# A state-space layer's dt and dt x, repeated through HBM in one transfer each

## The chip, the cores and the metric

The kernel runs on one core of a Trainium2 chip. The metric is the device time of one execution in microseconds. Engines are named as in the profile: PE is TensorE (PEld its weight loads), DVE is VectorE, ACT is ScalarE, POOL is GpSimd, SP is SyncE, which issues most DMAs.

## The reference

A decoder layer on x of 8 sequences of 512 tokens with 512 features, all in float32: a state-space (Mamba) block, a cross attention with 16 heads, and a mixture of 32 experts, each followed by a layer norm. The change lies in the state-space block, with 1024 channels d and 16 states n for each:

```python
dt = softplus(dt @ dt_proj_w + dt_proj_b)
dA = exp(A * dt[..., None])
dBx = dt[..., None] * B_ssm[:, :, None, :] * x_main[..., None]

def scan_fn(h, inp):
    dA_t, dBx_t, C_t = inp
    h = dA_t * h + dBx_t
    y_t = einsum('bdn,bn->bd', h, C_t)
    return (h, y_t)
```

So each channel's dt is needed for its 16 decays, and each channel's dt x for its 16 inputs.

## The kernel before

**Tiling.** The program has three parts: `layers` (state-space block, attention, gate and shared expert), `experts`, and `finish`. `layers` walks over 16 chunks, each half a sequence (T = 256 tokens), two chunks to a sequence. Beside the scan of one sequence stands the attention and the gate of the sequence before it (`units`), cut into small parts, and the projections of the next chunk.

**A chunk** has 32 steps (q, g, jj): q is one of four groups of 256 channels, g one of four groups of states, jj one half of the channels of q. In a step a tile h of 128 partitions holds, on four partition groups of 32, four states of the same 32 channels, and along the free axis four times 32 channels by 256 tokens. So 512 such steps make the layer. A step is
- `steps_in` (L497, VectorE): h = dt x times B, with B broadcast along partitions in a tile bc;
- `scan` (L504, VectorE): the recurrence along the tokens, with the decays in l_da, of which there are two;
- `collect` (L513, VectorE): h times C, in place;
- `products` (L524, PE): sums over the states of the four partition groups into py, through a matrix fold;
- for the next step, `carry` (L491, ACT: the first column of a new h) and `decays` (L483, ACT: four exponentials of dt);
- `keep` (L509, ACT) copies the last states of the chunk's first half, for the second.

The tile h comes from a pool with four buffers: the `steps_in` of a step waits for the `products` of four steps back.

**dt and dt x.** `prepare` (L440 to L463) makes dt and dt x of a q with 256 channels: a matmul, four kinds of ACT instructions, then four VectorE instructions (L460 to L463). These tiles have the channels on partitions. Since h has four copies of 32 channels, `repeat` (L432) copies rows of 32 partitions, 64 KB at a time and from SBUF to SBUF, into four tiles rep of 128 partitions (dt and dt x, for jj = 0 and 1): eight copies for a tile, 32 for a q. Each of the four has one buffer. `prepare` of a q stands at step 3 of the eight steps of the q before it; the `repeat` of dt at steps 5 and 6, that of dt x at steps 6 and 7.

**B and C.** `x_proj` leaves them in a small HBM tensor scr; `bcast` (L419) reads a row of it into 32 partitions at once, four copies for a tile bc.

**Order.** The Python text gives an order for each engine in which `part` and `run` put the side work into thirds of a step; `wait` delays the second half of a part by a step. The framework places instructions on each engine's queue, and the order on a queue is fixed when the program is built. An engine or a queue waits at its first instruction that isn't ready. SP issues the copies in such an order, and each waits for the copy eight before it on one of eight semaphores.

Of the kernel before, what the change touches and what calls it, by code (L numbers as in the profile page):

```python
# [8 lines left out]
F32 = mybir.dt.float32  # L9
# [8 lines left out]
P = 128  # L18
# [6 lines left out]
NST = 16  # L25
RANK = 32
CC = DI // P
T = 256
NT_ = T // P
NG = NST // 4  # L30
NQ = 4
QP = P // NQ
NB = 4
NPB = 3

# [53 lines left out]
def layers(ctx, tc, a, x1d, filld, based, xbuf):  # L89
# [23 lines left out]
    nc = tc.nc  # L113

    mp = ctx.enter_context(tc.tile_pool(name="l_mamba", bufs=1))
# [7 lines left out]
    dp = ctx.enter_context(tc.tile_pool(name="l_dram", bufs=2, space=DRAM))  # L123
# [289 lines left out]
    def bcast(f, g):  # L413

        got = []
        for r0 in (g, NST + g):
            t = bcp.tile([P, T], F32, tag="bc", name="bc")
            for s in range(NQ):
                nc.sync.dma_start(  # L419
                    t[s * QP : (s + 1) * QP], f["scr"][r0 + s * NG, :].partition_broadcast(QP)  # L420
                )
            got.append(t.unsqueeze(1).to_broadcast([P, NB, T]))
        f["bc", g] = got

    def repeat(f, q, what, jj):

        to = mp.tile([P, 2, 2, T], F32, tag=f"rep{what}{jj}", name="rep")
        src = f["ready", q][what]
        for s in range(NQ):
            for j in range(2):  # L430
                r0 = (2 * jj + j) * QP
                nc.sync.dma_start(to[s * QP : (s + 1) * QP, j], src[r0 : r0 + QP])  # L432
        f["rep", what, q, jj] = to

    def prepare(q, f):

        ps = psm.tile([P, 2, T], F32, tag="mm", name="ps_dt")
        for i in range(2):
            c = 2 * q + i
            nc.tensor.matmul(  # L440
                ps[:, i, :], w_dt[:, c * P : (c + 1) * P], f["xd"][0:RANK, :], start=True, stop=True
            )

        def exponentials():
            u = mp.tile([P, 2, T], F32, tag="u", name="u")
            dt = mp.tile([P, 2, T], F32, tag="dt", name="dt")

            for i in range(2):
                c = 2 * q + i
                nc.scalar.activation(u[:, i, :], ps[:, i, :], AF.Abs, bias=b_dt[:, c : c + 1])  # L450
                nc.scalar.activation(dt[:, i, :], ps[:, i, :], AF.Relu, bias=b_dt[:, c : c + 1])  # L451
            nc.scalar.activation(u, u, AF.Exp, scale=-1.0)
            l = mp.tile([P, 2, T + 3], F32, tag="xp", name="l")[:, :, 0:T]
            nc.scalar.activation(l, u, AF.Ln, bias=1.0)
            w = dtx = mp.tile([P, 2, T], F32, tag="dtx", name="dtx")
            nc.scalar.activation(w, u, AF.Identity, bias=1.0)

            def both():

                nc.vector.scalar_tensor_tensor(w, w, -1.0, u, ALU.add, ALU.subtract)  # L460
                nc.vector.tensor_tensor(l, l, w, ALU.subtract)
                nc.vector.tensor_tensor(dt, dt, l, ALU.add)
                nc.vector.tensor_tensor(dtx, dt, f["xs"][q], ALU.mult)  # L463
                f["ready", q] = dt, dtx
                return wait(timesD)

            def timesD():
                for i in range(2):
                    c = 2 * q + i
                    nc.scalar.activation(  # L470
                        f["xs"][q][:, i, :], f["xs"][q][:, i, :], AF.Identity, scale=dpar[:, c : c + 1]
                    )

            return wait(both)

        return exponentials
# [10 lines left out]
    def carry(t, q, g, jj):  # L487

        last = state[:, q, g, jj].unsqueeze(2)
        h = mp.tile([P, NB, T + 1], F32, tag="h", name="h", bufs=4)  # L490
        nc.scalar.copy(h[:, :, 0:1], last if t else nothing)  # L491
        return h

# [12 lines left out]
    def keep(t, q, g, jj, h):  # L506

        if t < S // T - 1:
            nc.scalar.copy(state[:, q, g, jj].unsqueeze(2), h[:, :, T : T + 1])  # L509
# [565 lines left out]
    f = {"xt": x0}  # L1075
# [13 lines left out]
    n = 0  # L1089
# [6 lines left out]
    nc.vector.tensor_scalar(aneg, aneg, -1.0, None, ALU.mult)  # L1096
    decays(f, 0, 0, 0, das[0])
    ahead, products = carry(0, 0, 0, 0), None
    old, side, cleared = None, [], 0
    clock.append(0)  # L1100

    for i, (b, t) in enumerate(chunks):
        nf = {}
        after = chunks[i + 1] if i + 1 < len(chunks) else None
        if t == 0:
            side, spent = units(b - 1) if b else sources(0), 0.0

            own = [work(k) for k in range(len(steps))] * 2
            whole = sum(own) + sum(x[0] for x in side)
        for k, (q, g, jj) in enumerate(steps):  # L1110
            if i and k == 1:
                bcast(f, NG - 1)
            if after and 28 <= k < 31:
                bcast(nf, k - 28)
            qf, nq = (f, q + 1) if q + 1 < CC // 2 else (nf, 0)
            h = ahead

            parts = []

            def part(fn, *args, first=False):  # L1120
                parts.append((do, fn, *args, first))

            if k in (2, 3) and old:
                part(back, k - 2, *old)
            if 4 <= k < 8:
                part(gate_x, k - 4, f)
            if k == 8:
                parts.append((finish_silu, f["zs"]))
            if k % 8 == 3:
                if q + 1 < CC // 2:  # L1130
                    part(prepare, q + 1, f)
                elif after:
                    part(prepare, 0, nf)
            if after:
                if k == 10:
                    part(norm_x, nf)
                if k == 13:
                    for j in range(DC // 2):
                        part(flip_x, j, nf)
                if k in (14, 16, 19, 22):  # L1140
                    part(convolve, after[1], (14, 16, 19, 22).index(k), nf, first=(k == 14))
                if k == 24:
                    parts.append((finish_silu, *nf["xs"].values()))
                if k == 25:
                    part(x_proj, nf)
            if side and (k >= 4 or t and k < 2):
                at = t * len(steps) + k + 1
                while side and spent + sum(own[:at]) <= whole * at / len(own):
                    w, fn, alone = side.pop(0)
                    spent += w  # L1150
                    part(fn, first=alone)
            thirds = [[], [], []]
            for m, x in enumerate(parts):
                thirds[round((m + 0.5) * 3 / len(parts) - 0.5) if x[0] is do else 1].append(x)

            def run(m):
                clock[0] += 1
                settle()
                for x in thirds[m]:
                    if x[0] is do:  # L1160
                        do(*x[1:-1], first=x[-1])
                    else:
                        x[0](*x[1:])

            steps_in(f, q, g, jj, h)
            if g == NG - 1 and (qf is f or after):
                repeat(qf, nq, 1, jj)
            if k % 8 == 1:
                if k > 1:
                    gated(q - 1, f)  # L1170
                elif old:
                    gated(CC // 2 - 1, old[2])
            if i == 0 and k == 0:
                load("Wo")
            if i == 0 and k == 2:
                biases()
            if k == 0 and old:
                twice_x(*old)
            if k == 7 and after:
                load_x(*after, nf)  # L1180
            run(0)
            scan(das[n % 2], h)
            n += 1

            if k + 1 < len(steps) or after:
                then = steps[(k + 1) % len(steps)]
                ahead = carry(t if k + 1 < len(steps) else after[1], *then)
                decays(f if k + 1 < len(steps) else nf, *then, das[n % 2])
                if k % 8 in (5, 6) and (qf is f or after):
                    repeat(qf, nq, 0, k % 8 - 5)  # L1190
            keep(t, q, g, jj, h)
            run(1)

            if products:
                products()
            products = collect(f, q, g, jj, h)
            run(2)
            while i < 2 and cleared < E * (i * len(steps) + k - 6) // (2 * len(steps) - 7):
                clear(cleared)
                cleared += 1  # L1200
        while t and side:
            _, fn, alone = side.pop(0)
            do(fn, first=alone)
        old = (b, t, f)
        f = nf
# [356 lines left out]
```

## Time and profile before

| | |
|---|---|
| median of 3 runs | 5823.85 us (5821.39 to 5825.35) |
| profiled execution | 5829.17 us |
| its span, first to last instruction | 5827.5 us |
| state-space stage (77 to 3975 us) | 3898 us |
| rest (experts, finish) | 1852 us |
| PE busy in the span | 4844.7 us (83%) |
| DVE busy in the span | 4256.2 us (73%) |
| ACT busy in the span | 2571.1 us (44%) |
| copies of L432 | 2048 of 64 KB |
| copies of L419 | 512 of 32 KB |

The stage holds 16 chunks of some 244 us. A row "engine line <- releaser: us, times, longest" of the waits tells how long an engine stood still before an instruction of that line, and what ended it; "DMA rep<-dtx" is a copy that landed. In the time line an instruction's start and duration come first, and the idle time before it last, in brackets.

### The profile page before, as it was taken

Reading aid. Unit: us, or ns where it says so; the run is one execution under the profiler, and the core shown is the slowest. Engines: PE = TensorE matmul, PEld = TensorE weight load, DVE = VectorE, ACT = ScalarE, POOL = GpSimd, SP = SyncE. Lnnn points to the kernel's source line nnn. Section 1 sums busy time; section 2 is a strip of 40 time slices with the busy share of each in tenths; the row PEclk is TensorE's granted clock in tenths of the full one; section 3 lists DMA queues with packets and bytes.
Section 4 is the critical chain, followed back from the end, with each engine's and each line's share of the span. In section 5 each row is a group of like instructions: output and inputs, shape, how many; then the busy total and the mean of one; then the engine's idle time right before and its main releaser. Section 6 shows DMA issues by size and latency. Waiting matters only on the chain. (4 is left out here: it accounts for less than half of the span.)

```text
span 5827.5 us, 56423 instructions
## 1 busy us (share of the span) xinstructions
PE 4844.7 (83%) x17320; PEld 2526.6 (43%) x17320; DVE 4256.2 (73%) x5372; ACT 2571.1 (44%) x5688; POOL 524.8 (9%) x424
## 2 busy tenths in 40 slices
PE   5556878888888888887788787878899999999995
PEld 3122323323333333332343243233377777777773
DVE  5877879788787987988778798876355555555554
ACT  4444555556455455645545555553222222222223
POOL 0000002000100100010020010001111111111111
PEclk7767889898989899898898898989899999999997
DMA  5566335424533543362443354244234444444444
GB/s 163 157 209 188 97 96 144 139 73 116 171 81 101 153 126 84 107 185 60 118 147 110 90 142 140 70 102 138 84 98 125 125 121 121 123 121 122 122 121 145
DMA packets 517407, 719.33 MB, mean 123 GB/s; under 512 B 148097, under 2 KB 231585, under 8 KB 515056
## 3 DMA queue, kind: packets, MB, share of 16 engines
q1 hardware_dynamic: 481088, 627.28, 36.3%
q0 software_dynamic: 33280, 76.90, 6.8%
q10 hardware_dynamic: 2736, 11.54, 0.5%
q8 instruction: 138, 2.26, 0.2%
q14 instruction: 165, 1.35, 0.1%
HBM read 391.24 MB, written 165.05 MB: 95 GB/s over the span
## 5 line engine op out<-in xcount | busy, mean ns | idle before, releaser
L504 DVE TENSOR_TENSOR_SCAN h<-l_da,h 128x1028 f32<-128x1028 f32 x512 | 1167.0, 2289 | 62.7 <-ACT l_da L483 58.2
L483 ACT ACTIVATE l_da<-rep,l_aneg 128x256 f32<-128x256 f32 x2048 | 886.2, 498 | 364.7 <-DVE h L504 342.6
L524 PE MATMUL py<-h,l_fold 128*32 128x512 f32 x2048 | 462.5, 692 | 510.5 <-DVE h L513 450.2
L497 DVE TENSOR_TENSOR h<-rep,bc 128x1024 f32<-128x1024 f32 x512 | 613.1, 1215 | 277.4 <-DMA rep<-dtx 126.2
L513 DVE TENSOR_TENSOR h<-h,bc 128x1024 f32<-128x1024 f32 x512 | 619.9, 1217 | 5.2
L818 DVE TENSOR_REDUCE mx<-ps_s 128x2 f32<-128x1024 f32 x256 | 310.6, 1217 | 207.3 <-PE ps_s L816 188.1
L1312 PE MATMUL ps_h<-xT,w 128*128 128x320 f32 x1536 | 436.0, 433 | 0.0
L816 PE MATMUL ps_s<-l_ka,l_qa 64*128 64x512 f32 x1024 | 371.4, 731 | 59.9 <-DVE mx L818 58.8
L524 PEld LDWEIGHTS py<-h,l_fold 128*32 128x32 f32 x2048 | 62.3, 114 | 783.3 <-DVE h L513 388.2
L1392 POOL DMA_INDIRECT based<-y,xe x160 | 256.5, 1603 | 1309.1 <-ACT y L1415 580.7
L842 PE MATMUL ps_t<-l_qa,l_ka 64*128 64x512 f32 x1024 | 332.6, 669 | 46.1 <-DVE mx L818 17.8
L1312 PEld LDWEIGHTS ps_h<-xT,w 128*128 128x128 f32 x1536 | 292.6, 191 | 118.3 <-issue 0.6
L1333 DVE TENSOR_TENSOR hT<-ps_h,p 128x320 f32<-128x320 f32 x128 | 62.9, 492 | 379.0 <-PE ps_h L1312 379.0
L846 ACT ACTIVATE eT<-ps_t 128x1024 f32<-128x1024 f32 x256 | 260.2, 1017 | 152.1 <-PE ps_t L842 151.2
L858 PE MATMUL po<-eT,l_va 128*64 128x512 f32 x1024 | 307.2, 657 | 13.3 <-ACT eT L846 13.3
L1312 PE MATMUL ps_h<-t,s 128*128 128x320 f32 x1024 | 286.1, 432 | 0.0
L691 POOL DMA_INDIRECT xbuf<-x2t,dest x128 | 212.7, 1662 | 676.5 <-DVE dest L682 610.3
L509 ACT COPY l_state<-h 128x4 f32<-128x4 f32 x256 | 50.0, 195 | 498.4 <-DVE h L504 497.2
L555 PE MATMUL po<-wm,zs 128*128 128x512 f32 x512 | 250.1, 635 | 13.8 <-ACT nm L829 9.7
L753 PE MATMUL ps_p<-x2T,wa 128*128 128x512 f32 x512 | 248.4, 638 | 12.0 <-DVE hT L945 8.0
L344 PE MATMUL ps_x<-xnT,wm 128*128 128x256 f32 x1024 | 248.7, 397 | 5.4 <-ACT dt L451 3.1
L344 PE MATMUL ps_z<-xnT,wm 128*128 128x256 f32 x1024 | 238.7, 392 | 15.3 <-DMA wm<-in_in_proj_w 14.6
(230 smaller groups left out, 7465.2 us busy)
## 6 DMA issues: line engine op xcount, KB each, us to landing
w<-in_w SPq DMA_DIRECT2D x93, 1024.0 KB
wm<-in_in_proj_w SPq DMA_DIRECT2D x128, 512.0 KB
rep<-dt SPq DMA_DIRECT2D x1024, 64.0 KB
rep<-dtx SPq DMA_DIRECT2D x1024, 64.0 KB
xbuf<-zero SPq DMA_DIRECT2D x32, 1362.5 KB
xe<-xbuf SPq DMA_DIRECT2D x32, 1362.5 KB
wm<-in_out_proj_w SPq DMA_DIRECT2D x64, 512.0 KB
wa<-in_sw SPq DMA_DIRECT2D x24, 1024.0 KB
```

The source lines that it names most:

```text
L344: nc.tensor.matmul(ps[:, i, :], w[:, dc, i * P : (i + 1) * P], f["xnT"][:, dc, :], start=(dc == 0), stop=(dc == DC - 1),)
L483: nc.scalar.activation(da[:, n, 1:], dt[:, j, i, :], AF.Exp, scale=aneg[:, 2 * q + i, 2 * jj + j, g : g + 1])
L497: nc.vector.tensor_tensor(h[:, :, 1:], dtx.rearrange("p j i t -> p (j i) t"), f["bc", g][0], ALU.mult)
L504: nc.vector.tensor_tensor_scan(flat, da.rearrange("p n t -> p (n t)"), flat, 0.0, ALU.mult, ALU.add)
L513: nc.vector.tensor_tensor(h[:, :, 0:T], h[:, :, 1:], f["bc", g][1], ALU.mult)
L524: nc.tensor.matmul(f["py"][j * QP : (j + 1) * QP, :, :], fold, hs[j // 2][:, 2 * (j % 2) : 2 * (j % 2) + 2, 0:T], start=False, stop=g == N ...
L816: nc.tensor.matmul(ps[:, j, :], qa[r, lt * P : (lt + 1) * P], ka[r, :], start=True, stop=True)
L818: return lambda: nc.vector.tensor_reduce(mx[:, lt, :].unsqueeze(2), ps, AX.X, ALU.max) and None
L842: nc.tensor.matmul(ps[:, j, :], ka[r, kc * P : (kc + 1) * P], qa[r, :], start=True, stop=True)
L846: nc.scalar.activation(eT, ps, AF.Exp)
L858: nc.tensor.matmul(po[j * 2 * HD : (j + 1) * 2 * HD, :], va[:, kc, i, j * HD : (j + 2) * HD], eT[:, j, :], start=(kc == 0), stop=(kc == SC ...
L1312: nc.tensor.matmul(ps, w[:, n, r * P : (r + 1) * P], x[:, n, :], start=not more and n == 0, stop=n == 1, skip_group_check=more,)
```

## The change

- `repeat` reads from HBM: when `prepare` has made dt and dt x, each is stored to HBM in two copies (one for each jj), and `repeat` then fills a tile rep of 128 partitions with one copy, whose source has a step of 0 over the four partition groups. Its four calls for a q now stand at steps 5 and 6.
- The tiles rep share five buffers, in turn, instead of one for each of four names.
- `bcast` fills a tile bc with one copy, whose source has the four groups of states in front and a step of 0 over 32 partitions.
- `prepare` stands at step 2 of eight (for the first q of the next chunk still at step 27 of the chunk).
- h has five buffers.
- `keep` of a step is called a step later, after the next step's `carry` and `decays`.

```diff
         for r0 in (g, NST + g):
             t = bcp.tile([P, T], F32, tag="bc", name="bc")
-            for s in range(NQ):
-                nc.sync.dma_start(
-                    t[s * QP : (s + 1) * QP], f["scr"][r0 + s * NG, :].partition_broadcast(QP)
-                )
+            src = f["scr"].rearrange("(n s g) t -> n g s t", n=2, s=NQ)[r0 // NST, r0 % NST]
+            nc.sync.dma_start(t, src.unsqueeze(1).to_broadcast([NQ, QP, T]))
...
-        to = mp.tile([P, 2, 2, T], F32, tag=f"rep{what}{jj}", name="rep")
-        src = f["ready", q][what]
-        for s in range(NQ):
-            for j in range(2):
-                r0 = (2 * jj + j) * QP
-                nc.sync.dma_start(to[s * QP : (s + 1) * QP, j], src[r0 : r0 + QP])
-        f["rep", what, q, jj] = to
+        f["rep", what, q, jj] = to = mp.tile([P, 2, 2, T], F32, tag="rep", name="rep", bufs=5)
+        src = f["ready", q][what][jj]
+        nc.sync.dma_start(
+            to.rearrange("p j i t -> p (j i t)"),
+            src.rearrange("c j f -> c (j f)").unsqueeze(0).to_broadcast([NQ, QP, 4 * T]),
+        )
...
-                f["ready", q] = dt, dtx
+                f["ready", q] = [dp.tile([2, QP, 2, 2 * T], F32, tag=n, name=n) for n in ("dtd", "dtxd")]
+                for to, src in zip(f["ready", q], (dt, dtx)):
+                    for r in range(2):
+                        nc.sync.dma_start(
+                            to[r].rearrange("c j f -> j c f"), src[r * HP : (r + 1) * HP].rearrange("p i t -> p (i t)")
+                        )
...
-        h = mp.tile([P, NB, T + 1], F32, tag="h", name="h", bufs=4)
+        h = mp.tile([P, NB, T + 1], F32, tag="h", name="h", bufs=5)
...
-            if k % 8 == 3:
-                if q + 1 < CC // 2:
-                    part(prepare, q + 1, f)
-                elif after:
-                    part(prepare, 0, nf)
+            if k % 8 == 2 and q + 1 < CC // 2:
+                part(prepare, q + 1, f)
+            if k == 27 and after:
+                part(prepare, 0, nf)
...
-            if g == NG - 1 and (qf is f or after):
-                repeat(qf, nq, 1, jj)
+            more = qf is f or after
+            if k % 8 == 6 and more:
+                repeat(qf, nq, 0, 1)
...
-                if k % 8 in (5, 6) and (qf is f or after):
-                    repeat(qf, nq, 0, k % 8 - 5)
-            keep(t, q, g, jj, h)
+                if k % 8 == 5 and more:
+                    repeat(qf, nq, 0, 0)
+                    repeat(qf, nq, 1, 0)
+                if k % 8 == 6 and more:
+                    repeat(qf, nq, 1, 1)
+            if held:
+                keep(*held)
+            held = t, q, g, jj, h
             run(1)
```

More of the change, by code (lines that the diff above doesn't have):

```diff
@@ L32 @@
 QP = P // NQ
+HP = P // 2
 NB = 4
@@ L1098, in layers @@
     ahead, products = carry(0, 0, 0, 0), None
-    old, side, cleared = None, [], 0
+    old, side, cleared, held = None, [], 0, None
     clock.append(0)
```

## The prediction

> **What bounds the kernel now.** I read the window sums first, to find the stage that the change touches; then VectorE's waits in it; then the time line around the longest of those waits. The change lies between 77 us (first scan product) and 3975 us (last scan). The windows of that stage and of the expert stage (columns: window, us, busy us and instructions of PE, PEld, DVE, ACT, POOL, granted clock, DMA share, GB/s):
>
> ```profile
> 77.00:3975.00 3898.00, 3057.89 (x10228) 1281.86 (x10230) 3219.52 (x3439) 2023.02 (x4566) 229.72 (x197) 0.87 0.43 125
> 3975.00:5827.00 1852.00, 1744.54 (x6956) 1216.47 (x6952) 1018.00 (x1884) 518.89 (x1064) 284.37 (x190) 0.97 0.45 121
> ```
>
> VectorE works 3220 of 3898 us, TensorE 3058: VectorE paces the stage, TensorE is close behind, and 678 us of VectorE's time is idle. A chunk (32 steps) takes 243.6 us, a step 7.6 us, of which a scan (2.29 us) and its two products (1.22 us each) are 4.7. VectorE's waits in the stage (total us, times, longest):
>
> ```profile
> DVE mx L818 <- PE ps_s L816: 144.7, 50, 10.0
> DVE h L497 <- DMA rep<-dtx: 126.2, 14, 25.2
> DVE h L497 <- PE py L524: 117.0, 62, 6.1
> DVE h L504 <- ACT l_da L483: 58.2, 31, 6.3
> ...
> DVE h L497 <- PE ps_p L753: 22.4, 2, 11.6
> ...
> DVE h L497 <- issue: 5.7, 1, 5.7
> DVE h L497 <- DMA rep<-dt: 5.4, 3, 4.9
> ```
>
> The waits at L497 other than for py stand at the starts of a q, where the repeated dt and dt x arrive: 159.7 us in all. One of them on VectorE and on SP's queue:
>
> ```profile
> 1545.96 0.67 DVE L463 TENSOR_TENSOR dtx<-dt,xs 128x512 f32<-128x512 f32 x1
> ...
> 1559.17 1.22 DVE L497 TENSOR_TENSOR h<-rep,bc 128x1024 f32<-128x1024 f32 x1 [11.27 <-DMA rep<-dtx]
> ```
> ```profile
> 1549.65 1.78 SPq L432 DMA_DIRECT2D rep<-dt  x3
> 1551.84 4.95 SPq L432 DMA_DIRECT2D rep<-dtx  x8
> ...
> 1558.23 3.23 SPq L432 DMA_DIRECT2D rep<-dt  x5
> ```
>
> Eight 64 KB copies cost SP 5 us, and a q needs four such groups: dt x is ready at 1546.6 and its first half is there at 1559.2, 12.6 us later. By the landing records in the trace a 64 KB copy lands 2.0 us after its issue, a 128x512 store to HBM 2.0 to 2.8, a 512 KB weight tile 4.5. The same start in odd chunks shows as a 10.0 us wait of mx for ps_s. Over a pair of chunks (eight q) these waits are 11.3 + 4.0 + 2.2 + 1.3 + 4.9 + 10.0 = 34 us.
>
> **The change part by part.** Only this stage changes; VectorE's and ScalarE's arithmetic stays.
>
> *SP's issues.* 2048 copies of 0.59 us (L432) become 256 stores and 256 reads; 512 row broadcasts become 128. SP is relieved of some 900 us of issue. That is worth nothing by itself: it counts only through when data arrive.
>
> *When they are needed.* From the instruction order of the changed program and the durations above, VectorE's work between the dt x product and the first product that needs it (the cover) is, for the eight q of a pair from an even chunk's q = 1, 6.9, 10.4, 19.5, 9.1, 1.6, 16.2, 20.6, 6.8 us (before: 1.6, 15.8, 16.0, 19.5, 2.3, 17.6, 16.9, 14.2). The second product, which needs the other half, stands 2.5 us later. `prepare` a step earlier thus gives 5 us at one q and takes some elsewhere.
>
> *How long the new path takes: the row.* No row shows such a store and read. Nearest: two stores issued (0.7), landed (2.0 to 2.8), a read issued (0.6) and landed (4.5): 8 us after the dt x product. The stalls of a pair would be 1.1 + 0 + 0 + 0 + 6.4 + 0 + 0 + 1.2 = 9 us instead of 34.
>
> *The rule against it.* The Trainium skill, "DMA: Bandwidth & Descriptors", section "Why a DMA increments its semaphore by 16 and not by 1", says that a copy runs on at most 16 engines, and on the largest number up to 16 that divides the slowest dimension of both access patterns; its "Rules for kernel authors" warn of just this case, "a leading zero-stride broadcast of c copies". The built patterns: a read has source [4 copies, 32, 1024], so 4 engines; a store has destination [2, 32, 512], so 2; a row broadcast has source [4, 32 copies, 256], so 4. All copies of before had 32 or 128 in front. This trace agrees as far as it can: the six l_ka<-l_ones copies, with 4 in front, add to their semaphore once and then four times singly, where rep's copies add sixteen times. But those have only four rows, so no row shows many rows on four engines.
>
> By the rule the sum is another. An undisturbed packet of 2048 bytes takes 84 ns in this trace, one of 4096 bytes 159 ns. A store is 64 rows on 2 engines, 32 x 84 ns = 2.7 us on each; a read is 128 rows on 4 engines, 32 x 159 = 5.1 us. They share the first engines of one queue, so they follow each other there. With dt ready at 0, dt x at 1.0, and 1.65 us of fixed latency (2.0 less a 64 KB copy's four packets): stores end at 4.4, 7.1, 9.8, 12.5; reads at 17.6, 22.7, 27.8, 32.9. So the first half of dt x lands 21.7 us after the dt x product, the second 31.9. What stands between in SP's order (weight tiles 1.4 us each on an engine, attention rows) adds 1.4 to 4; the other traffic's share of an engine, 0.43 of the window less 0.13 for rep and bc (65,536 packets of 110 ns and 16,384 of 51 ns on 16 engines in 3898 us), would stretch 31.9 to 46 if it fell evenly. I take 35, near the lower end, since that traffic comes in bursts. Stalls of a pair at 35, with covers 2.5 us longer than above: 25.6 + 22.1 + 13.0 + 23.4 + 30.9 + 16.3 + 11.9 + 25.7 = 169 us.
>
> I take the rule: the page is specific, its count agrees with the small copies, and the built patterns are exactly those that it names. Its price is the likeliest, the row's is a rival.
>
> *Five h, later copies of the last states.* Before, the write to h waits 117 us for the py matmul four steps back; a fifth buffer puts the awaited matmul a step, some 5 us of VectorE's work, further back; between nothing and all 117 I take 65, as PE stays late at its own lumps. The held copy no longer makes ScalarE wait for the scan (497 us, mostly time in which ScalarE had nothing else); for VectorE I count at most 20 of its 58 us on l_da. What is late next is ps_s and py. When VectorE stalls 20 us at a q, TensorE catches up, and part of these gains and of the other waits (678 - 160 - 70 - 117 = 331 us, 41 a pair) is inside the stall; I take 20 of them and 8 of py a pair.
>
> *SP waits.* A read waits for its store, and behind it on SP stand weight tiles, kd/qT rows, nm and x1d; all use the crowded engines too. Demand on engine 0 for a q: four reads 20.4, four stores 10.8, two row broadcasts 3, others 0.30 x 61 = 18 us, together 52 of 61 us: tight, not yet the bound. Weight tiles are loaded three ahead and attention rows two head pairs ahead, which covers 15 to 20 us; without it TensorE would wait inside VectorE's stall.
>
> *Sum against the profiled execution (5829.2 us; span 5827.5).* A pair: +169 - 34 - 8 - 20 = +107; eight pairs +860. The first pair has DMA shares of 0.60 and 0.65 from the clearing of xbuf: +60 more. The start is about even (before, the first product comes 28 us after dt x; here some 32). Together +920: 6749, and as the median of the runs lies 5 us below the profiled time, 6745.
>
> **The rivals.**
> 1. *All 16 engines serve the new copies* (0.11). For it: no row of before contradicts it, and SP's issue, the visible cost, falls. Then 160 + 70 (mx) - 70 (stalls of 9 us a pair) + 65 + 20 = 245 us are freed; TensorE works 200 of 243.6 us a chunk, so a third returns as waits for it: -165, 5660 us. This ends faster. The deciding point is the landing of the second half: at 21 us after the dt x product the stalls are 60 us a pair, about what goes with the old path (34) and what is gained or lies inside the stalls (28). Below it faster, above it slower.
> 2. *Only the reads are confined, the stores are spread* (part of 0.87). Stores then take 3 us, the second half lands at 24.5: stalls 85 a pair, 85 - 62 = +23 a pair, with the first pair's 60 about 6070 us.
> 3. *The first engines become the bound* (part of 0.87). If the other traffic stretches the path to 45 us, the stalls are 249 a pair, 249 - 62 = +187 a pair: about 7300 us and TensorE starts to wait for wm.
> 4. *Gains and stalls cancel* (0.02).
>
> **How the numbers follow.** Confined engines 0.87, of which the middle case is the likeliest: 6745. Spread over 16: 0.11. The range runs from rival 2 to a little above rival 3, 6050 to 7400; it leaves out rival 1 and a tail of long queueing. Runs of before lie within 4 us of each other, so 0.2% (12 us) can be told. Faster 0.10, same 0.02, slower 0.88.
>
> **What would show it.** Right: waits "DVE h L497's product <- DMA rep<-dtxd" of over 1000 us in the stage, some 20 us at nearly each of 64 q, most at an odd chunk's q = 1; VectorE's busy time unchanged at 3220 us in a longer stage; expert stage still 1852 us; DMA share not above 0.43, though transfers are late; lower TensorE share. Wrong: reads that land within 6 us of their issue, and L497's waits under 100 us.

## The result, and the profile after

The changed kernel takes 6572.4 us (median of 4 runs, 6567.1 to 6579.6) against 5824.6 us (4 runs): ratio 1.1282, 95% interval 1.1263 to 1.1302. The profiled execution took 6572.3 us, 743 us more than that of before. The same parts of the page and of the window sums as before; the windows are cut so that the second is as long as before (the last scan ends at 4703 us, 15 us ahead of that cut):

```profile
PE 4969.2 (76%) x17320; PEld 2562.1 (39%) x17320; DVE 4224.3 (64%) x5372; ACT 2560.6 (39%) x5700; POOL 513.7 (8%) x424
...
HBM read 525.46 MB, written 198.61 MB: 110 GB/s over the span
```
```profile
83.00:4718.00 4635.00, 3185.06 (x10236) 1317.63 (x10237) 3186.99 (x3437) 2011.83 (x4574) 226.93 (x202) 0.82 0.35 112
4718.00:6570.00 1852.00, 1741.82 (x6947) 1215.06 (x6945) 1014.38 (x1880) 518.20 (x1064) 276.12 (x185) 0.97 0.46 120
```

From the first scan product to the end of the last scan the stage grew from 3899 to 4621 us, 722 of the 743 us; it starts 5 us later, and what follows the last scan takes 1868 us instead of 1851. VectorE's busy time in the stage did not grow (3187 us in the first window, before 3220), so its idle time did: 1448 us instead of 678. The DMA share fell from 0.43 to 0.35: on average over the 16 engines there is more room than before, while VectorE waits for copies. VectorE's waits (us in total, times, longest):

```profile
DVE h L500 <- DMA rep<-dtxd: 1078.4, 118, 23.1
DVE z L963 <- DMA based<-z: 102.8, 6, 19.3
DVE h L500 <- PE py L527: 72.6, 32, 6.9
...
DVE mx L821 <- PE ps_s L819: 47.1, 12, 7.7
DVE h L507 <- ACT h L494: 33.0, 7, 5.8
...
DVE h L507 <- ACT l_da L486: 8.2, 7, 2.8
```

L500 is the product that was L497. Its wait for dt x was 126 us and is 1078. The second row is new: a store of another part of the layer, z to HBM, now holds VectorE. Others shrank (ps_s 145 to 47, py 117 to 73, l_da 58 to 8), which fits that they lie inside the long waits. ScalarE stands as long for the copies of dt:

```profile
ACT l_da L486 <- DMA rep<-dtd: 1144.7, 124, 21.5
```

That is not what holds VectorE: its scan waits only 8 us for l_da, as dt x lands later than dt. One start of a q on VectorE and on SP's queue:

```profile
2092.21 0.69 DVE L460 TENSOR_TENSOR dt<-dt,l 128x512 f32<-128x512 f32 x1
...
2095.09 0.67 DVE L461 TENSOR_TENSOR dtx<-dt,xs 128x512 f32<-128x512 f32 x1
...
2119.18 2.36 DVE L500 TENSOR_TENSOR h<-rep,bc 128x1024 f32<-128x1024 f32 x2 [22.15 <-DMA rep<-dtxd]
...
2129.90 1.23 DVE L500 TENSOR_TENSOR h<-rep,bc 128x1024 f32<-128x1024 f32 x1 [6.15 <-DMA rep<-dtxd]
```
```profile
2092.96 1.20 SPq L465 DMA_DIRECT2D dtd<-dt  x2
...
2095.78 2.59 SPq L465 DMA_DIRECT2D dtxd<-dtx  x2
2098.42 1.50 SPq L428 DMA_DIRECT2D rep<-dtd  x1
2106.36 0.56 SPq L428 DMA_DIRECT2D rep<-dtxd  x1
2107.03 0.51 SPq L428 DMA_DIRECT2D rep<-dtd  x1
2108.93 1.21 SPq L428 DMA_DIRECT2D rep<-dtxd  x1
```

dt x is ready at 2095.8. SP issues the first read of it at 2106.4, after its store has landed, and all four reads by 2110. The first product starts at 2119.2 and the first one of the second half at 2129.9, 34 us after dt x. So the time goes into the copies themselves. Over the steady part (q 8 to 63) the trace's semaphore records give these means, from the dt x product on: stores landed after 6.7 (dt) and 13.3 us (dt x), the first half of dt x after 26.0, the second after 37.8. In the kernel before the two halves were there after 14.9 and 26.6 us.

The same records tell how many engines carry a copy. A read (rep) adds 5 times to its semaphore, a store 3 times, a row broadcast (bc) 5 times; the copies that had 32 or 128 rows in front add 16 times. The first addition of a dt x read comes 1.0 us after its issue, the other four 13 us and later (medians). Read as one addition at the issue and one for each engine, this is 4, 2 and 4 engines.

The copies that are still spread over 16 engines show the same without that reading. In the kernel before, the 16 additions of a store of z come between 2.1 and 2.6 us after its issue (in order, medians over the stores with all 16 on record). In the changed kernel twelve come after 5.3 to 5.4 us, two after 12 and two after 18. So four engines are late, and two of them later still: this is what to expect if the 2 engines of the stores are among the 4 of the reads.

### The profile page after: what moved, and what is told of

The parts are those of the page before. It is cut to its first block, busy times and chain, and to the rows that moved or that the text cites. A ratio compares the mean times of both kernels' runs of the same rounds, so it can differ in the third digit from the quotient of the medians.

```text
span 6570.6 us, 53769 instructions
## 1 busy us (share of the span) xinstructions
PE 4969.2 (76%) x17320; PEld 2562.1 (39%) x17320; DVE 4224.3 (64%) x5372; ACT 2560.6 (39%) x5700; POOL 513.7 (8%) x424
## 5 line engine op out<-in xcount | busy, mean ns | idle before, releaser
L500 DVE TENSOR_TENSOR h<-rep,bc 128x1024 f32<-128x1024 f32 x512 | 616.2, 1215 | 1164.4 <-DMA rep<-dtxd 1078.4
L845 PE MATMUL ps_t<-l_qa,l_ka 64*128 64x512 f32 x1024 | 356.6, 762 | 294.4 <-ACT eT L849 234.4
L527 PE MATMUL py<-h,l_fold 128*32 128x512 f32 x2048 | 428.1, 661 | 174.4 <-DVE h L516 141.1
L819 PE MATMUL ps_s<-l_ka,l_qa 64*128 64x512 f32 x1024 | 333.4, 724 | 204.0 <-DVE mx L821 188.5
L861 PE MATMUL po<-eT,l_va 128*64 128x512 f32 x1024 | 345.4, 754 | 65.2 <-ACT eT L849 51.2
L558 PE MATMUL po<-wm,zs 128*128 128x512 f32 x512 | 281.1, 707 | 144.6 <-DVE z L963 122.5
L345 PE MATMUL ps_z<-xnT,wm 128*128 128x256 f32 x1024 | 259.3, 413 | 81.8 <-ACT zs L391 60.0
L756 PE MATMUL ps_p<-x2T,wa 128*128 128x512 f32 x512 | 262.5, 668 | 58.7 <-ACT hT L950 50.9
L845 PEld LDWEIGHTS ps_t<-l_qa,l_ka 64*128 64x128 f32 x1024 | 113.0, 222 | 464.7 <-ACT eT L849 277.4
L345 PEld LDWEIGHTS ps_z<-xnT,wm 128*128 128x128 f32 x1024 | 208.9, 208 | 155.8 <-ACT zs L391 72.5
L819 PEld LDWEIGHTS ps_s<-l_ka,l_qa 64*128 64x128 f32 x1024 | 92.3, 206 | 391.0 <-DVE mx L821 285.9
```

What stands on the lines that cost most here:

```text
L345: nc.tensor.matmul(ps[:, i, :], w[:, dc, i * P : (i + 1) * P], f["xnT"][:, dc, :], start=(dc == 0), stop=(dc == DC - 1),)
L500: nc.vector.tensor_tensor(h[:, :, 1:], dtx.rearrange("p j i t -> p (j i) t"), f["bc", g][0], ALU.mult)
L527: nc.tensor.matmul(f["py"][j * QP : (j + 1) * QP, :, :], fold, hs[j // 2][:, 2 * (j % 2) : 2 * (j % 2) + 2, 0:T], start=False, stop=g == N ...
L558: nc.tensor.matmul(pos[j], yg[:, c, j * P : (j + 1) * P], w[:, i, :], start=(c == 0), stop=(c == CC - 1))
L819: nc.tensor.matmul(ps[:, j, :], qa[r, lt * P : (lt + 1) * P], ka[r, :], start=True, stop=True)
L845: nc.tensor.matmul(ps[:, j, :], ka[r, kc * P : (kc + 1) * P], qa[r, :], start=True, stop=True)
```

## The experiments

Line numbers shift by a few between kernels. In what follows "the product" is that of `steps_in`.

**1. All three copies spread over 16 engines, the way through HBM kept.** Channels and states stay where they were in the partitions; the copies are cut so that 32 rows stand in front.

```diff
-        nc.sync.dma_start(
-            to.rearrange("p j i t -> p (j i t)"),
-            src.rearrange("c j f -> c (j f)").unsqueeze(0).to_broadcast([NQ, QP, 4 * T]),
-        )
+        for s in range(NQ):
+            nc.sync.dma_start(
+                to[s * QP : (s + 1) * QP].rearrange("p j i t -> p (j i t)"), src.rearrange("c j f -> c (j f)")
+            )
...
-                        nc.sync.dma_start(
-                            to[r].rearrange("c j f -> j c f"), src[r * HP : (r + 1) * HP].rearrange("p i t -> p (i t)")
-                        )
+                        for j in range(2):
+                            r0 = r * HP + j * QP
+                            nc.sync.dma_start(to[r][:, j, :], src[r0 : r0 + QP].rearrange("p i t -> p (i t)"))
```

(The row broadcasts go back to four copies each.)

> The changed kernel with each of its new copies cut so that 32 rows stand in front on both sides: a tile rep by four reads of 32 rows of 4 KB, a tensor by four stores, a tile bc by four copies; the way through HBM, the five tiles rep and h and the later keep stay. Theory (few engines serve the new copies): all of them now run on 16 engines, each should add to its semaphore sixteen times, the first half of dt x lands some 8 to 12 us after the dt x product instead of 26, the waits of L500's products for rep fall from 1078 us to under 200, and the time is 5600 to 5800 us. Rival (the way through HBM, a store that has to land before a read starts, is itself the cost): 6300 us or more.

Measured: 6046.5 us, ratio to before 1.0369 (1.0351 to 1.0386). VectorE's waits in its stage:

```profile
DVE mx L823 <- PE ps_s L821: 166.8, 61, 10.4
DVE zs L543 <- ACT zs L396: 141.5, 9, 21.6
DVE xs L379 <- ACT xs L371: 123.7, 38, 13.1
...
DVE h L502 <- DMA rep<-dtxd: 27.9, 4, 13.0
```

The wait for dt x falls from 1078 to 28 us, as the theory said, and all these copies now add 16 times. But the first half of dt x is there after 16.8 us, not 8 to 12, and the time is in neither range: other waits, for TensorE and ScalarE, come up, and the kernel is 4% slower than before. With the engines spread the waits for rep are gone, yet this kernel, with 16 reads for a q, loses time in another way, and late work elsewhere probably hides part of what rep would still cost. Experiments 2 and 8 bear on it.

**2. The same engines with few copies: channels interleaved.** Channel c and state s go to partition 4c + s instead of 32s + c. Then the source of a read has 32 channels in front and the 4 repeats behind, and one copy goes to 16 engines. `fold` and the layout of A follow; the row broadcasts have 32 in front as well; the stores are cut as in experiment 1.

```diff
-            src.rearrange("c j f -> c (j f)").unsqueeze(0).to_broadcast([NQ, QP, 4 * T]),
+            src.rearrange("c j f -> c (j f)").unsqueeze(1).to_broadcast([QP, NQ, 4 * T]),
```

> Partition 4c + s instead of 32s + c: the source of a read is 32 channels in front, then a step of 0 over four, so a tile rep and a tile bc are still filled by one copy, on 16 engines; the stores are cut in four of 32 rows. VectorE's instructions stand in the same order as in spread_stores, so the two differ only in the engines of the reads. Theory: 5600 to 5750 us, as fast as spread_all or faster, for SP issues fewer copies. Rival (the way through HBM): 6300 us or more. Rival (a single large copy is slow because of its size): as slow as spread_stores.

Measured: 5429.6 us, ratio to before 0.9315 (0.9300 to 0.9331): faster than both kernels, and than the theory's range. Its page's engines, and VectorE's waits in the stage:

```profile
PE 4738.2 (87%) x17320; PEld 2491.1 (46%) x17320; DVE 4217.5 (78%) x5372; ACT 2560.8 (47%) x5703; POOL 542.1 (10%) x424
```
```profile
DVE h L501 <- DMA rep<-dtxd: 74.3, 20, 10.9
DVE h L501 <- PE py L528: 61.0, 22, 7.5
...
DVE mx L822 <- PE ps_s L820: 37.9, 24, 4.6
```

A read of dt x lands 6.1 us after its issue (median; 18 in the changed kernel), a cut store 1.7. The two halves of dt x are there 11.6 and 16.5 us after the product that makes it (26.0 and 37.8 in the changed kernel). The way through HBM, the five tiles, the earlier prepare and the single reads are all still there. What changed is the order of the dimensions and the cut of the stores.

**3. Stores alone spread** (experiment 1's edit to the stores, reads and row broadcasts as in the changed kernel, on 4 engines).

> The changed kernel with its stores alone cut in four of 32 rows (16 engines); reads and row broadcasts stay on four. Theory: stores land some 3 us after the dt x product instead of 13.3; four reads of 5.1 us follow each other on the same engines, so the first half of dt x lands after about 14 us and the second after 25; some half of the loss goes: 5950 to 6200 us. Rival (the way through HBM): within 100 us of 6570.

Measured: 6081.5 us, ratio 1.0429 (1.0411 to 1.0446), inside the theory's range, though the halves of dt x are there later than it had them, after 20.2 and 31.8 us. VectorE, ScalarE and TensorE have the same instructions in the same order as in experiment 2, so the step from here to experiment 2, 652 us, is the price of reads and row broadcasts on 4 engines instead of 16.

```profile
DVE h L500 <- DMA rep<-dtxd: 707.4, 103, 17.7
```

**4. Stores alone confined:** experiment 2 with the changed kernel's two stores for each tensor.

```diff
-                        for j in range(2):
-                            r0 = r * HP + j * QP
-                            nc.sync.dma_start(to[r][:, j, :], src[r0 : r0 + QP].rearrange("p i t -> p (i t)"))
+                        nc.sync.dma_start(
+                            to[r].rearrange("c j f -> j c f"), src[r * HP : (r + 1) * HP].rearrange("p i t -> p (i t)")
+                        )
```

> The interleaved kernel (channel c and state s in partition 4c+s; reads and row broadcasts on 16 engines; 5430 us) gets back the changed kernel's stores, two copies for each of dt and dt x with 2 in front of 32 rows, thus on 2 engines. With the changed kernel (stores 2, reads 4: 6572 us), the one with spread stores (16, 4: 6081 us) and the interleaved one (16, 16: 5430 us) it completes a square. Theory (the copies of the few engines follow each other there, so the cost is the sum of rows ahead of the last half, less the cover by other VectorE work): stores alone end 8.8 and 11.5 us after dt x, reads of 5 us then land at 14 and 17 us, against covers of 6.9, 10.4, 19.5, 9.1, 1.6, 16.2, 20.7, 6.8 us that makes some 35 us a pair of chunks, 280 in all, less the 77 us of rep waits that the interleaved kernel has: 5600 to 5750 us. Rival (the two losses add up): 5430 + 491 = about 5920 us. Rival 2 (the reads' engines alone matter): 5430 to 5480 us.

Measured: 5745.4 us, ratio 0.9856 (0.9839 to 0.9872), inside the theory's range.

```profile
DVE h L501 <- DMA rep<-dtxd: 296.7, 42, 14.6
```

The square is complete (device us; waits of the product for dt x in brackets):

| | reads on 4 engines | reads on 16 |
|---|---|---|
| stores on 2 engines | 6572 (1078) | 5745 (297) |
| stores on 16 | 6081 (707) | 5430 (77) |

Spreading the reads is worth 827 or 652 us, the stores 491 or 316. ("Reads" includes the row broadcasts.) The effects are not additive: waiting that one copy causes is partly shared with the other. Along each row VectorE and ScalarE have the same instructions in the same order, so there the engines of the copies are the whole difference for them. Down a column the built order differs too (some 4,600 of VectorE's 5372 instructions stand in the same order), so 491 and 316 hold that as well.

**5. The suspected cost doubled:** experiment 3 with each tile filled by two copies that have 2 in front.

```diff
-        nc.sync.dma_start(
-            to.rearrange("p j i t -> p (j i t)"),
-            src.rearrange("c j f -> c (j f)").unsqueeze(0).to_broadcast([NQ, QP, 4 * T]),
-        )
+        for s in range(0, NQ, 2):
+            nc.sync.dma_start(
+                to[s * QP : (s + 2) * QP].rearrange("p j i t -> p (j i t)"),
+                src.rearrange("c j f -> c (j f)").unsqueeze(0).to_broadcast([2, QP, 4 * T]),
+            )
```

> The kernel with the stores in four copies of 32 rows (6081 us) is changed in one thing: each tile rep is filled by two copies whose source has 2 copies in front of 32 rows, so that by the rule a read runs on 2 engines instead of 4. Theory (a confined copy's rows are worked off one after the other by its few engines, in the same first engines each time): a read tile then costs the first two engines 64 rows x 0.162 us = 10.4 us instead of 5.2, four tiles of a q 41 us instead of 21, so the second half of dt x lands some 20 us later and the first some 10; with the other traffic the first two engines are asked for 60 to 65 us of work in a q's 61 us, so they become the bound of the stage: 7000 to 7500 us, waits for rep<-dtxd over 1500 us, semaphore adds of 3 for each read copy. Rival 1 (the two copies of a tile are put on different pairs of engines, so the row count matters and not where the rows go): 6050 to 6150 us. Rival 2 (the loss came from the way through HBM and from the number of issues): also 6050 to 6150, with waits for rep near the 707 us of the four-engine kernel.

Measured: 7113.0 us, ratio 1.2207 (1.2187 to 1.2228). The reads add 3 times to their semaphores.

```profile
DVE h L501 <- DMA rep<-dtxd: 1570.6, 127, 32.9
```

The theory's numbers came in: the halves of dt x are there after 30.1 and 51.7 us, 9.9 and 19.9 later than in experiment 3 (10 and 20 were expected). Both rivals, near 6100 us, are out. Had the two copies of a tile gone to different pairs, each tile would still have been spread over four engines in all. The additions of z's stores show where the copies went: fourteen come by 6.6 us, the last two after 19 and 20, where experiment 3 has four late ones (15.5 to 16.7). They stack up on the same two.

**6. Five h and the later `keep` alone,** in the kernel before.

```diff
-        h = mp.tile([P, NB, T + 1], F32, tag="h", name="h", bufs=4)
+        h = mp.tile([P, NB, T + 1], F32, tag="h", name="h", bufs=5)
...
-            keep(t, q, g, jj, h)
+            if held:
+                keep(*held)
+            held = t, q, g, jj, h
```

> The kernel before with five tiles h and keep a step later alone. Prediction's term: the waits for py fall by some 65 of 117 us and 20 us on l_da go, of which two thirds are kept: 5750 to 5800 us. Rival (VectorE comes earlier to the same late rep copies, as the order gives them less work to hide behind): no change or slower, 5820 to 5900 us.

Measured: 5839.5 us, ratio 1.0016 (1.0006 to 1.0027): no gain.

```profile
DVE mx L818 <- PE ps_s L816: 192.3, 68, 11.4
DVE h L497 <- DMA rep<-dtx: 136.1, 22, 24.6
...
DVE xs L378 <- ACT xs L370: 80.9, 29, 13.1
DVE h L504 <- ACT l_da L483: 76.2, 56, 6.3
```

The rival's range holds it. The rows are of the whole span, where the kernel before has 188, 126, 52 and 58 us. In the stage the product's wait for py, 117 us before, is 3 us; but xs went from 37 to 67, l_da from 58 to 76, and the wait of zs (L538) for py from 21 to 50. VectorE reached the next late thing earlier.

**7. The same two parts taken out of experiment 2** (four h, `keep` at once).

> The interleaved kernel (5430 us) with four buffers h and the last states copied in the same step, as in the kernel before: this prices these two parts of the change where the copies are no longer late. Theory (the fifth h pays only where VectorE is not held up elsewhere): in the kernel before it brought nothing (5839 for 5830 us); here VectorE is the pace, TensorE at 87% is close, so waits of the product for py come back, 61 us to 100 to 200 us, and the time is 5470 to 5560 us. Rival (what is gained at py is lost at ps_s again, as in the kernel before): 5415 to 5445 us.

Measured: 5409.0 us, ratio 0.9289 (0.9270 to 0.9307). The intervals of this and of experiment 2 overlap: no difference that can be told. It lies a little under both ranges. The py wait is 88 us instead of 61, less than expected, and the wait for dt x 39 instead of 77. Together with experiment 9 this stays without a settled sign.

**8. Reads on 8 engines:** experiment 2 with four copies for a tile, each with 8 channels in front.

```diff
+        for c in range(0, QP, 8):
+            nc.sync.dma_start(
+                to[NQ * c : NQ * (c + 8)].rearrange("p j i t -> p (j i t)"),
+                src[c : c + 8].rearrange("c j f -> c (j f)").unsqueeze(1).to_broadcast([8, NQ, 4 * T]),
+            )
```

> The interleaved kernel (reads on 16 engines, 5430 us) with each tile rep filled by four copies whose source has 8 channels in front of the 4 repeats, so that by the rule a read runs on 8 engines: with 2 engines 7113 us and 4 engines 6081 us (both with spread stores) it gives the row of 2, 4, 8, 16. SP issues 16 reads for a q instead of 4 (7 us more of issue). Theory (the engines set the landing, 128 rows of 0.16 us shared among them): 8 engines need 2.6 us a tile instead of 5.2, the second half of dt x lands about 11 us after the first read's issue instead of 21: 5500 to 5700 us, nine adds to a semaphore for a copy of 8 engines. Rival (anything less than all 16 engines jams the first ones): 5900 us or more. Rival 2 (8 engines are as good as 16 and the issues are hidden): 5400 to 5470 us.

Measured: 5980.1 us, ratio 1.0261 (1.0243 to 1.0279). The time is in the first rival's range (5900 us or more), but not for its reason, and the profile shows that it prices no engines. A read adds 9 times, thus 8 engines; z's stores have eight additions by 3.2 us and eight by 5.5, so nothing is jammed; and the waits for dt x are 129 us instead of 77, 52 of the 550 us by which the kernel is slower than experiment 2. The rest is what experiment 1 showed. TensorE's largest wait in the stage, in this kernel and then in experiment 2:

```profile
PE py L529 <- DVE h L518: 448.8, 82, 14.2
```
```profile
PE py L528 <- DVE h L517: 112.1, 48, 6.7
```

TensorE stands four times as long at the sums py, up to 14 us each, because h isn't ready; what stands behind them on its queue (ps_s, ps_x, ps_l) is then late for VectorE: 171 us at ps_s, 132 at xs. In experiment 1 the same wait is 521 us. Both kernels issue 16 reads for a q where experiment 2 issues 4, and both were built with another order of instructions: only some 3,700 of VectorE's 5372 stand in the order of experiment 2. So the number of copies also changes the order on the other engines. That this order, and not SP's longer issue, causes the loss was not separated.

**9. Fewer, larger stores, smaller reads:** experiment 2 with one store of 128 rows for each tensor, and two reads for each tile.

```diff
-                    for r in range(2):
-                        for j in range(2):
-                            r0 = r * HP + j * QP
-                            nc.sync.dma_start(to[r][:, j, :], src[r0 : r0 + QP].rearrange("p i t -> p (i t)"))
+                    nc.sync.dma_start(to, src.rearrange("p i t -> p (i t)"))
...
+        for j in range(2):
+            nc.sync.dma_start(
+                to[:, j].rearrange("p i t -> p (i t)"), src[j].unsqueeze(1).to_broadcast([QP, NQ, 2 * T])
+            )
```

> The interleaved kernel (5430 us) with one store of 128 rows for each of dt and dt x (16 engines) instead of four of 32 rows, and each tile rep filled by two reads of 2 KB rows (16 engines) instead of one of 4 KB rows. SP issues 2 stores and 8 reads for a q instead of 8 and 4. Theory (what remains is the sum of issues and landings on SP's queue before the first half of dt x): stores are issued 3.6 us earlier (6 issues of 0.6 us fewer), the reads land as before, 5 to 6 us after their issue: rep waits fall from 77 to under 50 us, 5390 to 5430 us. Rival (TensorE at 87% has become the pace and the rep waits were taken up by others): 5420 to 5450 us whatever the copies do. Rival 2 (four more reads of half the size cost more than the stores save): 5440 to 5500 us.

Measured: 5371.5 us, ratio 0.9218 (0.9202 to 0.9233), the fastest of all; 7.8% under the kernel before. The time is a little under the theory's range, its reason did not hold: the waits for dt x rose from 77 to 122 us, and those for ps_s fell from 83 to 52 over the span. Two more versions of it were run, the first with four h and `keep` at once, the second with prepare at step 3 besides:

> The interleaved kernel with one store for each tensor and two reads for each tile (5371 us), with four buffers h and the last states copied in the same step as before (which alone took the interleaved kernel from 5430 to 5409 us). Theory (five h and the later copies bring nothing and cost a little through ScalarE and the order of instructions): 5340 to 5365 us. Rival (what it brought there was the order of that one build): 5365 to 5400 us.

> The kernel of one store, two reads and four h, with prepare back at step 3 of eight (step 27 stays for the next chunk's first q). Between the dt x product and the first product that needs it VectorE then has, by the order of instructions, 10, 10, 15, 16, 6.5, 12, 12, 13 us of work for the eight q of a pair of chunks, in place of 5.5, 12, 30, 16, 7, 24, 23, 7.5; the first half of dt x lands some 8 to 9 us after the dt x product (store 2.1, issues 2 to 3, read 4.4). Theory (what counts is the smallest covers, and these grow): rep waits fall by 30 to 60 us in all, 5310 to 5360 us. Rival (the earlier prepare is what the fast path needs): 5380 to 5450 us.

Measured: 5437.9 us (ratio 0.9327, 0.9314 to 0.9340) and 5420.7 us (0.9299, 0.9286 to 0.9312). With four h the py wait goes from 61 to 148 us and the time up by 66, against both expectations; in experiment 7 it did not. The earlier prepare is not needed here: put back, the waits for dt x fall from 66 to 39 us, and the time by 17 us; the total lies in that rival's range only because four h had cost 66. Each of these edits also changes the order that is built, and moves of 1% between such versions can't be given to one part.

**10. The row broadcasts alone back to 16 engines,** in the changed kernel.

> The changed kernel (6572 us) with the row broadcasts alone put back to four copies of 32 rows (16 engines): 512 copies of 0.5 us on SP instead of 128. Theory (these 256 KB-per-q copies are a small part of what the four engines carry, 3 of some 50 us a q): 6480 to 6570 us. Rival (the short broadcasts also stand ahead of the stores and reads in the same queue and more issues delay SP): 6570 to 6650 us.

Measured: 6597.3 us, ratio 1.1320 (1.1300 to 1.1340), just above the changed kernel's 1.1282. The theory's small gain did not come; the rival's range holds it. A row broadcast lands in 1.9 us (5.2 in the changed kernel), 512 are issued instead of 128, and the waits for dt x are 1117 us (1078). Spreading the broadcasts alone gains nothing.

## Why the prediction was right, and where its sizes were off

- **The side and the cause: right.** Copies of a few engines hold up dt x. The Trainium skill's rule in "DMA: Bandwidth & Descriptors", section "Why a DMA increments its semaphore by 16 and not by 1" (the largest number up to 16 that divides the slowest dimension of both patterns) gives 4, 2 and 4, and the semaphores add 5, 3 and 5 times. With the order of dimensions changed (and the stores cut), the same way through HBM is 7% faster than before instead of 13% slower.
- **What would show it: nearly all came.** Waits over 1000 us (1078, 118 times), VectorE's busy time unchanged, a lower DMA share (0.35), a lower share of TensorE, the longest stalls at an odd chunk's q = 1 (29 us in the mean). The rest, 1868 us after the last scan, is 16 us longer.
- **The landing: too early.** 21.7 and about 35 us were worked out; 26.0 and 37.8 were measured. The packet term was right (4096 bytes: 162 ns in the median, 159 taken), but the stores land after 13.3 us where 11.5 were worked out, and the other traffic probably costs the first half as well, to which no allowance was given. (A 64 KB copy is 32 packets, two for each of 16 engines, where the fixed latency was worked out with four; that is under 0.2 us.)
- **The stalls: too long, and the term that made the sum miss.** 169 us a pair and 60 for the first were worked out, 1412 in all; 1078 were measured. Over pairs of the steady part (q 9 to 56) the trace has 135 a pair, 94 before first halves and 41 before second ones. What was mis-sized is the step "The second product, which needs the other half, stands 2.5 us later". By the semaphores that each product waits for, at five of the eight q another product of the first half comes ahead of it, and its covers are 12.2, 15.6, 27.2, 18.5, 6.3, 24.4, 25.6, 12.2 us: 142 a pair, where 111 were taken. Some 31 more a pair go into other waits of VectorE that stand between dt x and its first product, 17 of them in the wait of z for its store, at an even chunk's first q; the sum did not take them off. These two terms lower the stalls by some 62 us a pair; the later landing puts about 22 back: 129, near the 135.
- **What the stall swallows: right in size.** Besides the old waits for rep (132 us), 140 of the q-start waits and 28 a pair of others were to vanish, 364 us. From the rows of both traces the waits that shrank (ps_s 98, l_da 50, py 44, and o, zs, g_m, ps_p, dtx, ps_t about 145) make some 337.
- **Waits that were not counted:** z for its store to HBM, 103 us, and the scan for the carried column of h, 33 us. The first is the crowding: that store lands in 19.1 us (median; 2.8 before).
- **Five h and the later copies:** "I take 65" for py and 20 for l_da in the freed case. Experiment 6 gives nothing in the kernel before: the waits moved to ps_s and xs. In the sum for the changed kernel this term was small (the 8 us of py a pair).
- **The rivals.** "All 16 engines" is the machine of experiment 2, where 5660 was worked out and 5430 measured. 245 us were to be freed and a third of the gain to return as waits for TensorE; instead VectorE's idle time in the stage fell by 362 us (678 to 316), as waits of which the sum counted little or nothing shrank too (l_da 58 to 8, o 37 to under 1, xs 37 to 4). Its granted TensorE clock in the stage was 0.90, before 0.87, which may be part of it. "Only the reads are confined", 6070, is experiment 3: 6081. That agreement is in part luck, as the second half was there after 31.8 us and not 24.5. As an answer to what this change does, both are out by the semaphore counts. "The engines become the bound" was not reached at 4 engines; 7113 us at 2 comes near its 7300, but whether the two engines are then the bound was not measured.

The sum, +920 against +743, thus has 334 us too much for dt x and about 150 too little for waits elsewhere: two errors that partly cancel.

## What to carry to other kernels

Before you replace many small copies by one, look at the slowest dimension of both of its access patterns: with 2, 4 or 8 there, copies ran here on 2, 4 or 8 engines, and it was worth 652 to 827 us to have 32 channels in front of the 4 repeats instead of behind, by choosing the partition layout. In a profile it shows as transfers that land late while the DMA share is low; count a copy's additions to its semaphore. And before you sum a stall, take from the built order which instruction needs which half, and expect a changed number of copies to change the order elsewhere.

## What the runs showed of the hardware

- **A few crowded engines delay copies that use all 16.** In the changed kernel stores and loads that were spread as before landed late: z to HBM 19.1 us after its issue (2.8 before), x1d 21 (3.3), and one in_proj weight tile in ten took over 17 us (6), at a DMA share of 0.35. Twelve of x1d's sixteen additions come after 7.1 to 7.3 us, two after 16 to 17, two after 21 (medians): the copy is complete only with the last.
- **Confined copies share the same engines.** The number of late additions of z's store follows the number of engines of the confined copies: four with reads on 4 (experiment 3), two with stores on 2 (experiment 4) or reads on 2 (experiment 5), two and two with reads on 4 and stores on 2, none that stands apart in experiment 2 (5.9 to 7.2 us). Doubling the rows for each engine (experiment 5) took the time from 6081 to 7113 us.
